# A graph-attention kernel on one core: two groups of nodes share one row of chunks

## The chip, the core and the metric

The kernel runs on one core of a Trainium2 chip. The core has five engines, each with its own queue of instructions that it works through in order: PE (matrix products; the profile lists its weight loads apart, as PEld), DVE (vector work), ACT (activation functions and copies), POOL (general work, and here the issue of gathers), and SP, which issues most plain transfers. They wait for one another by semaphores. Transfers run on 16 DMA engines. PE, DVE and ACT can read and write PSUM, the memory in which matrix products accumulate; all engines work on SBUF. Times are device microseconds of one execution. The time before is 2453.34 us, the median of three runs (2437.25 to 2455.11).

## The reference, cut to what matters

4096 nodes with 512 features pass through three attention layers over one sparse graph. An entry of the adjacency matrix is 1 with a probability that falls with both indices, so low nodes have many neighbours and high ones few. Each layer replaces a node's row by the softmax-weighted mean of its neighbours' projected rows:

```python
x = _layernorm(x + _L0_gnn_ref(x, adj, L0_gnn_W, L0_gnn_a), axis=-1)
x = _layernorm(x + _L1_gnn_ref(x, adj, L1_gnn_W1, L1_gnn_a1, L1_gnn_Wo, L1_gnn_ao, L1_gnn_lin1_w, L1_gnn_lin1_b, L1_gnn_lin2_w, L1_gnn_lin2_b), axis=-1)
...
def _gat_heads(x, adj_mask, W, a):
    Wh = jnp.einsum('nf,hfo->hno', x, W)
    src = jnp.einsum('hno,ho->hn', Wh, a[:, :O])
    dst = jnp.einsum('hno,ho->hn', Wh, a[:, O:])
    e = jax.nn.leaky_relu(src[:, :, None] + dst[:, None, :], ALPHA)
    e = jnp.where(adj_mask[None, :, :], e, NEG)
    attn = jax.nn.softmax(e, axis=-1)
    return jnp.einsum('hnm,hmo->hno', attn, Wh)
...
h = jax.nn.elu(_gat_heads(x, mask, W1, a1))
x1 = jnp.transpose(h, (1, 0, 2)).reshape(x.shape[0], -1)
h2 = _gat_heads(x1, mask, Wo[None], ao[None])[0]
out = jax.nn.elu(h2)
out = jax.nn.relu(out @ lin1_w + lin1_b)
return out @ lin2_w + lin2_b
```

`_L0_gnn_ref` is such a layer with 8 heads of 64, `_L1_gnn_ref` has one with 8 heads of 64 and one with a single head of 512, then two dense products (512 to 1024 to 512). A node without neighbours gets the mean of all rows.

## The kernel before

`sparse_path` works on lists of edges. (`dense_path`, the same computation without lists, runs only if a flag says that some list did not fit.)

**Tiles, groups and chunks.** The 4096 nodes are 32 tiles of 128. A tile has two groups of 64 nodes (`HN`). The edges of a group are laid one after the other into chunks of 128 places. The sizes are set when the program is built: `Part` (line 71) takes the expected number of edges of a group plus 4.2 standard deviations and rounds up to whole chunks, `chunks[h]`; `pairs` is the larger of the two. Tile 0 is cut into four parts by columns, all other tiles are one part, which makes 35 parts. Places that hold no edge are holes. Over all parts the chunks of both groups are 339, the pairs 181. Tile 1 has 12 and 10 chunks, tile 11 5 and 5, tile 31 3 and 3; each part of tile 0 has 9 and 4 or 9 and 5.

**Finding edges** (`find_edges`, line 796). For each part the adjacency rows are turned into signs (ACT), PE makes keys of them (L820, L821), and DVE takes the eight largest over and over (L827, L842), which gives a list of up to `k` neighbours per node. `k` runs from 104 or 112 for tile 0 down to 24. POOL and ACT make degrees (L854), the place at which each node's edges begin (`prs`, a matmul with the triangle `before`, L873) and `s1` (L884): for each chunk a matrix of 128 nodes by 128 places that says which node a place belongs to. Three matmuls per pair of chunks (L902 to L904) then fill `pl`, a PSUM tile with a single buffer, with each place's list, its position in it and its node; L904 adds the constant `own_b`. From `pl` come `nl` (the node of a place), `hole`, and on DVE `sel` and `src`, by which `idx`, the row to be gathered, is made. With `k` under 100 three DVE operations do this for a group of chunks (L912 to L919); in tile 0 there is one operation for each chunk (L925), in 20 groups for its four parts. At the end `limits` (L940, L942) hold the room of each part for the flag. Beside this, `beside(t)` projects tile t for the first layer. The weights of that projection are prepared early by products on POOL (`sprod`, L639) and reductions on DVE (L644). The order of instructions in this stage is set by the build's own scheduler.

**The two head layers** (`heads_layer`, line 1190) run one after the other with the same code, and the order of their instructions is written out by hand. Tiles go from 31 down to 0. The chunks of a tile are cut into units of at most 6 (`GC`): first the pairs that both groups have, then what only one group has. This makes 74 units. For each unit

- `gather` (line 992) has POOL issue one indirect DMA per chunk (L997): 128 rows of the projected table, chosen by `idx`. Rows past the table are left out, so holes move no bytes. There are seven buffers (`GB`), and the gathers of unit i+7 stand behind the work of unit i.
- `weights` (line 1054) makes the attention logits on DVE (`z`, L1065 to L1067: add, leaky maximum, subtract) and their exponents on ACT.
- `add` (line 1082) makes `sm` on DVE (L1093), 128 places by 64 nodes per chunk, multiplies the gathered rows by their weights (`g`, L1124), and sums them on PE into `acc` (L1115), each chunk into the 64 rows of its group.

Once per tile, `spread` (line 1006), two tiles ahead, makes the source nodes' scores of all places on PE and reduces them on DVE (L1035, `ls` L1048). It works in cuts of eight pairs; all cuts but the last are reduced on the spot, the last one later. A finished tile is divided by its sums, gets its layernorm (first layer) or elu (second), and is projected into the table of the next layer (L669). The next layer's gathers begin when the last row of that table is written.

**The third layer** gathers in the same way with four buffers (`GT`), makes `sm` with the weight in it, one DVE operation per chunk (L1102), and works off the two dense products (L1395, L1407) in pieces between the units: `due` grows with the chunks done, at most to 2.5, and each whole number lets a piece go. `fold` finishes a tile when the next tile's first unit is through, `turn` transposes it at the unit after that.

## Time and profile before

The profiled execution took 2276.34 us, with a span of 2274.6 us from its first to its last instruction. All rows below are of this execution.

| stage | us from the span's start | busy PE | DVE | POOL | mean granted clock of PE |
|---|---|---|---|---|---|
| finding edges | 0 to 531 | 367.64 | 379.91 | 220.96 | 0.83 |
| first head layer | 531 to 1016 | 353.61 | 389.48 | 343.62 | 0.90 |
| second head layer | 1016 to 1502 | 362.99 | 331.62 | 354.67 | 0.87 |
| third layer, gathers | 1502 to 2158 | 576.92 | 239.07 | 342.45 | 0.94 |
| third layer, end | 2158 to 2275 | 97.86 | 31.79 | 0.18 | 0.94 |

Over the whole span PE is busy for 1759.0 us, DVE for 1371.9, ACT for 669.2 and POOL for 1261.9. In the profile's lines "out<-in" names what an instruction writes and reads, L997 is a line of the kernel, and "<-" before an engine names what ended a wait. An engine's busy share is an average; whether it sets the pace of a stage is seen from whether it waits there.

### The profile page before, as it was taken

What the parts mean: (1) busy time and instruction counts of PE and PEld (TensorE: products, weight loads), DVE (VectorE), ACT (ScalarE), POOL (GpSimd) and SP (SyncE); (2) the same over time, 40 slices, a digit from 0 to 9 for tenths busy, and PEclk for the clock granted to TensorE, in tenths of its full rate; (3) what the DMA queues carried; (4) which work ended last, traced back from release to release, by engine and by line L of the source; (5) the groups of instructions that cost most, each with busy time, mean ns of one, the idle gap of its engine ahead of it and who ended that gap; (6) DMA issues with size and microseconds to landing.
All of it is one profiled execution on the core that took longest, in us unless ns stands there. A gap on an engine that the chain in (4) does not pass through costs nothing.

```text
span 2274.6 us, 29820 instructions
## 1 busy us (share of the span) xinstructions
PE 1759.0 (77%) x9024; PEld 1033.3 (45%) x9049; DVE 1371.9 (60%) x3750; ACT 669.2 (29%) x2361; POOL 1261.9 (55%) x1816
## 2 busy tenths in 40 slices
PE   3887866673887876756888777638989989898997
PEld 2665532221555554424665444325454544444444
DVE  5887777674999986746787767524242424433423
ACT  3345766664232221102443222012111111111111
POOL 5514443446777777737777777655546544444400
PEclk9898987775999997887999888869989999999999
DMA  6434555543777776625666666455345534434301
GB/s 213 126 113 144 217 201 195 212 148 106 226 229 230 230 221 196 170 78 157 174 174 176 180 186 180 118 167 148 90 139 135 167 103 119 126 99 132 101 19 43
DMA packets 139791, 352.02 MB, mean 155 GB/s; under 512 B 49122, under 2 KB 50154, under 8 KB 135654
## 3 DMA queue, kind: packets, MB, share of 16 engines
q0 software_dynamic: 81360, 206.30, 33.7%
q1 hardware_dynamic: 58262, 143.72, 18.1%
q8 instruction: 75, 1.23, 0.2%
q14 instruction: 94, 0.77, 0.1%
HBM read 371.18 MB, written 42.24 MB: 182 GB/s over the span
## 4 chain that ended last, share of the span: by engine, by line
PE 25%; issue 13%; DVE 13%; DMA 10%; POOL 10%; ACT 1%; POOLq 0%; DVEq 0%; SPq 0%; ACTq 0%
POOL g L997 9%; PE p L1395 9%; DMA g<-table_t,idx 9%; PE acc L1115 9%; DVE g L1124 4%; PE p L1407 3%; PE ph L669 3%; DVE bs L1173 1%; DVE sm L1093 1%; DMA xr<-sx_d 1%; DVE o L1152 1%; DVE z L1065 1%; DVE z L1066 1%; PE pt L655 1%; DVE z L1067 1%
## 5 line engine op out<-in xcount | busy, mean ns | idle before, releaser
L997 POOL DMA_INDIRECT g<-table_t,idx x1017 | 1029.9, 1013 | 558.1 <-issue 253.5
L1115 PE MATMUL acc<-g,sm 128*64 128x260 f32 (+2 forms) x4068 | 608.2, 435 | 252.4 <-DVE g L1124 202.3
L1115 PEld LDWEIGHTS acc<-g,sm 128*64 128x64 f32 x4068 | 351.8, 154 | 482.2 <-DVE g L1124 236.4
L669 PE MATMUL ph<-sw_t,xt 128*128 128x264 f32 (+1 forms) x1536 | 396.1, 407 | 48.0 <-ACT xt L658 36.8
L1124 DVE TENSOR_TENSOR g<-g,wp 128x2048 f32<-128x2048 f32 (+4 forms) x148 | 383.3, 2590 | 12.3 <-ACT wp L1072 12.3
L669 PEld LDWEIGHTS ph<-sw_t,xt 128*128 128x128 f32 x1536 | 295.0, 199 | 113.9 <-ACT xt L658 53.1
L827 DVE MAX8 cand<-key 128x8 f32<-128x24 f32 (+54 forms) x467 | 197.3, 446 | 88.7 <-PE key L821 86.3
L1395 PE MATMUL p<-sht,sl1w 128*128 128x512 f32 (+1 forms) x576 | 229.1, 553 | 0.0
L1407 PE MATMUL p<-sl2w,shid 128*128 128x512 f32 x512 | 228.2, 600 | 0.0
L658 ACT ACTIVATE xt<-pt 128x128 f32<-128x128 f32 x384 | 101.0, 278 | 218.8 <-PE pt L655 218.3
L1065 DVE TENSOR_TENSOR z<-s,g 128x48 f32<-128x48 f32 (+6 forms) x222 | 41.3, 186 | 202.1 <-DMA g<-table_t,idx 199.5
L1395 PEld LDWEIGHTS p<-sht,sl1w 128*128 128x128 f32 x576 | 108.1, 191 | 110.9 <-issue 105.9
L1407 PEld LDWEIGHTS p<-sl2w,shid 128*128 128x128 f32 x512 | 95.6, 191 | 120.1 <-issue 119.3
L820 PE MATMUL key<-sg,s_identb 128*128 128x512 bf16 (+1 forms) x255 | 120.6, 474 | 30.1 <-DVE cand L827 23.2
L682 ACT COPY hrow<-ph 128x260 f32<-128x260 f32 (+2 forms) x194 | 71.0, 373 | 183.0 <-PE ph L669 181.3
L1398 ACT ACTIVATE shid<-p,sl1b 128x512 f32<-128x512 f32 (+1 forms) x72 | 46.0, 639 | 250.7 <-PE p L1395 250.7
L793 ACT ACTIVATE sg<-raw 128x4096 bf16<-128x4096 int32 (+1 forms) x39 | 116.9, 2998 | 9.6 <-PE key L820 5.0
L1102 DVE TENSOR_SCALAR sm<-iota_n,nl,w 128x64 f32<-128x64 f32 x339 | 83.9, 325 | 50.7 <-ACT w L1075 50.7
L821 PE MATMUL key<-frac,places 128*128 128x512 bf16 (+1 forms) x236 | 111.4, 473 | 2.1 <-POOL places L756 2.0
L1169 DVE SCALAR_TENSOR_TENSOR o<-ex,o 128x512 f32<-128x512 f32 x64 | 44.2, 690 | 100.9 <-ACT ex L1168 100.7
L1072 ACT ACTIVATE wp<-z 128x32 f32<-128x32 f32 (+4 forms) x148 | 30.5, 206 | 231.3 <-DVE g L1124 231.1
L658 ACT ACTIVATION_READ_ACCUMULATOR xt<-pt 128x1 f32 x384 | 80.0, 208 | 0.0
(168 smaller groups left out, 1862.9 us busy)
## 6 DMA issues: line engine op xcount, KB each, us to landing
raw<-in_adj_dram SPq DMA_DIRECT2D x31, 2048.0 KB, 7.6
table_t<-hrow SPq DMA_DIRECT2D x64, 260.0 KB, 3.4
xr<-in_x_dram SPq DMA_DIRECT2D x64, 256.0 KB, 4.1
g<-table_t,idx POOLq DMA_INDIRECT x1017
table_t<-hrow SPq DMA_DIRECT2D x32, 257.0 KB, 3.8
sx_d<-o SPq DMA_DIRECT2D x32, 256.0 KB, 3.6
xr<-sx_d SPq DMA_DIRECT2D x32, 256.0 KB, 4.1
out_dram<-xr SPq DMA_DIRECT2D x32, 256.0 KB, 2.8
```

Of the source, the lines that this page charges most:

```text
L658: nc.scalar.activation(xt[:, c, :], pt[:, c, :], AF.Copy, accum_out=st.xparts[:, c, t : t + 1])
L669: nc.tensor.matmul(ph[:n], columns(c), st.w[:, c, j], start=(c == 0), stop=(c == FC - 1))
L793: nc.scalar.activation(sg[:, ts(i, w)], raw[:, ts(i, w)], AF.Sign)
L820: nc.tensor.matmul(out_, ident_b, sg[:, j:e], start=True, stop=False)
L821: nc.tensor.matmul(out_, places[:, w], frac[:, j - w * KW : e - w * KW], start=False, stop=True)
L827: nc.vector.max(out=cand[:, at : at + 8], in_=part)
L997: nc.gpsimd.indirect_dma_start(out=u.g[:, k, : self.st.row], out_offset=None, in_=self.st.table[:, :], in_offset=bass.IndirectOffsetOnAxis ...
L1102: nc.vector.tensor_scalar(sm[:, k], iota_n, node[:, i, h : h + 1], u.w[:, k], op0=OP.is_equal, op1=OP.mult)
L1115: nc.tensor.matmul(out_[h * HN : (h + 1) * HN], sm[:, k], rows(k), start=flags[k][0], stop=flags[k][1])
L1124: nc.vector.tensor_mul(body, body, wp[:, :, :, None].to_broadcast(body.shape))
L1395: nc.tensor.matmul(p1, l1w[:, c, ts(k, P)], hts[b][:, c, :n], start=(c == 0), stop=(c == FC - 1))
L1407: nc.tensor.matmul(p2, hids[b][:, k, ts(j, P)], l2w[:, k, :], start=(k == 0), stop=(k == HC - 1))
```

## The change

The two groups of a part now lie in one row of `n` chunks. Group 0 is laid from the front, group 1 so that it ends at the row's end, beginning in chunk `off`. The chunks in the middle hold edges of both. `n` comes from the edges of both groups together:

```diff
+        room = lambda lam: math.ceil((lam + 4.2 * math.sqrt(lam)) / P)
+        self.n = room(sum(lams))
+        self.chunks = [min(room(lam), self.n) for lam in lams]
+        self.blocks = max(self.chunks)
+        self.off = self.n - self.chunks[1]
```

Over all parts that is 309 chunks, and so 309 gathers per layer, for 339. The parts of tile 0 go from 13 and three times 14 to 12 and three times 13; tile 1 from 22 to 21, tiles 2 to 10 by one each, tile 11 from 10 to 8, tiles 12 and 13 stay at 8, tiles 14 to 19 go from 8 to 7, tiles 20 and 21 from 8 to 6, tile 22 from 7 to 6, tiles 23 to 28 stay at 6, tiles 29 to 31 go from 6 to 5. A chunk in the middle is gathered once and summed twice, so the sums over `sm` and `acc` stay at 339 slots per layer.

A unit takes chunks from the front and from the end; only the last of a part is one run:

```diff
+    def units(self):
...
+        a, b, out = 0, self.n, []
+        steps = math.ceil(self.n / GC)
+        size = min(max(1, round(self.n / steps / 2)), GC // 2)
+        for _ in range(steps - 1):
...
+            out.append(([(a, size), (b - size, size)], list(range(size)), list(range(size, 2 * size))))
+            a, b = a + size, b - size
...
+        out.append((
+            [(a, b - a)],
+            list(range(min(self.chunks[0], b) - a)),
+            list(range(max(self.off, a) - a, b - a)),
+        ))
```

This makes 66 units for 74. Tiles 20, 21 and 22 become one unit of 6 each; tiles 14 to 19 are units of 4 and 3.

In finding edges, `s1` keeps 181 blocks; block i serves chunk i for group 0 and chunk `off` + i for group 1. Group 1's places are counted back from the end (`mids`, `ends_at`). The constant now opens a group of chunks, and the blocks are added to it:

```diff
-                for c in range(m):
-                    chunk = s1[:, (c0 + lo + c) * P : (c0 + lo + c + 1) * P]
-                    nc.tensor.matmul(pl[:, c], chunk, rhs, start=True, stop=False)
-                    nc.tensor.matmul(pl[:, c, :, : k + 1], chunk, rest, start=False, stop=False)
-                    nc.tensor.matmul(pl[:, c, :, k:], ident_b, own_b, start=False, stop=True)
+                nc.tensor.matmul(
+                    pl, ident_b, own_b[:, None, kmax - k :].to_broadcast([P, m, k + 2]), start=True, stop=False
+                )
+                last = None
+                for block, groups, chunks in blocks_in(p, lo, m):
+                    for of, w in ((rhs, k + 2), (rest, k + 1)):
+                        if last:
+                            nc.tensor.matmul(*last, start=False, stop=False)
+                        last = pl[:, chunks, :w], s1[:, ts(p.at + block, P)], of[:, groups, :w]
+                nc.tensor.matmul(*last, start=False, stop=True)
...
-                        for h in range(2):
-                            nc.vector.scalar_tensor_tensor(
-                                sel[:, c, h], iota_k[:, lo + c, :k], kk[:, c, h : h + 1], pl[:, c, h, :k],
+                        nc.vector.scalar_tensor_tensor(
+                            sel[:, c], iota_k[:, lo + c, :k], kk[:, c : c + 1], pl[:, c, :k],
...
+    def blocks_in(p, lo, m):
...
+        for i in range(p.blocks):
+            mine = [(g, c - lo) for g, c in enumerate((i, p.off + i)) if i < p.chunks[g] and lo <= c < lo + m]
+            if len(mine) == 2:
+                out.append((i, slice(0, 2), slice(mine[0][1], mine[1][1] + 1, p.off)))
+            elif mine:
+                g, c = mine[0]
+                out.append((i, slice(g, g + 1), slice(c, c + 1)))
```

The constants by part are filled with one memset for each run of equal values, in place of one or two for each part. A check is added that both groups together fit:

```diff
+        def by_parts(name, of, rows=slice(0, P), rest=None):
...
+            while v < len(pts):
+                e = v
+                while e < len(pts) and of(pts[e]) == of(pts[v]):
+                    e += 1
+                nc.gpsimd.memset(out_[rows, v:e], float(of(pts[v])))
+                v = e
...
-        for v, p in enumerate(pts):
-            nc.gpsimd.memset(limits[0][:, v : v + 1], p.k - 0.5)
-            for h in range(2):
-                nc.gpsimd.memset(limits[1][h * HN : (h + 1) * HN, v : v + 1], float(p.chunks[h] * P))
```

`spread` makes its scores per part in cuts of 20 chunks, three values per head and place in place of four; the holes open the sum and the blocks are added:

```diff
-                pss = self.ps.tile([P, 8, 2, 4, hs], F32, name="pss")
+                pss = self.ps.tile([P, 20, 3, hs], F32, name="pss")
...
+                todo = blocks_in(p, lo, m)
+                for block, groups, chunks in todo:
                     nc.tensor.matmul(
...
-            for lo in cuts[:-1]:
-                collect(lo, scores(lo))
-            last = scores(cuts[-1])
+            cuts = [(p, lo) for p in parts_of(t) for lo in range(0, p.n, 20)]
+            for cut in cuts[:-1]:
+                collect(*scores(*cut))
+            last = scores(*cuts[-1])
```

`weights` adds and subtracts once for each run of a unit, and `add` makes `sm` in two operations, one for each group:

```diff
-            nc.vector.tensor_add(zd, s, d)
+            for at, s in u.pick(self.s[u.t], base):
+                nc.vector.tensor_add(zd[:, at], by(s), d[:, at])
             nc.vector.scalar_tensor_tensor(z, z, ALPHA, z, op0=OP.mult, op1=OP.max)
-            nc.vector.tensor_sub(zd, zd, ls)
+            for at, ls in u.pick(self.ls[u.t], base):
+                nc.vector.tensor_sub(z[:, at], z[:, at], ls)
...
+            for g, slots in enumerate(u.slots):
+                of_g = iota_n[:, g * HN : (g + 1) * HN]
+                if hs > 1:
...
+                    nc.vector.tensor_tensor(
+                        sm[:, at : at + n_],
+                        of_g[:, None, :].to_broadcast(shape),
+                        nl[:, c : c + n_, None].to_broadcast(shape),
+                        op=OP.is_equal,
                     )
```

In the third layer a tile of one unit can now be the last of the order, so what `fold` left is turned after the loop:

```diff
+        if folded:
+            turn(*folded)
         at.inverse(sb, order[-1])
```

## The prediction

> **What bounds the kernel now.** I read the page's groups first, to see what the removed instruction costs, then the busy time by stage, the waits inside each stage, and the order of time on single engines. By their first and last gathers the stages lie at 0 to 531 us (finding edges), 531 to 1016 (first head layer), 1016 to 1502 (second) and 1502 to 2275 (third layer with the dense blocks).
>
> The page's costliest group (busy us, mean ns | idle before, its cause):
>
> ```profile
> L997 POOL DMA_INDIRECT g<-table_t,idx x1017 | 1029.9, 1013 | 558.1 <-issue 253.5
> ```
>
> The answer for its source line (minimum, median and maximum ns of one):
>
> ```profile
> L997 POOL DMA_INDIRECT g<-table_t,idx x1017: 992/998/1527, 533.0 to 2157.2; - x170
> ```
>
> 1017 gathers are 339 per layer. Busy times between the first and last gather of each layer (PE, PEld, DVE, ACT, POOL, granted clock, DMA share, GB/s):
>
> ```profile
> 531.00:983.00 452.00, 332.89 (x2135) 218.72 (x2136) 376.13 (x725) 117.72 (x587) 343.61 (x341) 0.90 0.71 208
> 1016.00:1466.00 450.00, 341.86 (x2143) 222.88 (x2143) 320.06 (x542) 122.88 (x581) 346.75 (x340) 0.88 0.65 172
> 1502.00:2158.00 656.00, 576.92 (x2479) 308.09 (x2480) 239.07 (x891) 110.80 (x264) 342.45 (x340) 0.94 0.44 125
> ```
>
> POOL looks only 76% busy in the first two, but in order of time its gathers stand 0.30 us apart with nothing waited for:
>
> ```profile
> 668.37 0.99 POOL L997 DMA_INDIRECT g<-table_t,idx  x1 [0.30 <-issue]
> 669.67 1.00 POOL L997 DMA_INDIRECT g<-table_t,idx  x1 [0.30 <-issue]
> ```
>
> The pitch is 1.302 us. 339 x 1.302 = 441 us, and gathers ran from 533.0 to 983.0, 450 us: POOL is 98% of that stretch. In the second layer 441 of 447. The waits inside the three stretches confirm it:
>
> ```profile
> POOL g L997 <- PE acc L1115: 7.0, 11, 3.9
> ...
> DVE z L1065 <- DMA g<-table_t,idx: 96.4, 41, 11.2
> ...
> POOL g L997 <- PE acc L1115: 212.0, 47, 11.9
> ```
>
> First layer: POOL waited 7.0 us for buffers. Second: DVE waited 96.4 us for gathers. Third: the reverse, POOL waits 212 us for PE, which is busy 577 of 656 us. So a removed gather is worth up to 1.302 us in two layers and little in the third, as long as DVE, 83% busy in the first layer, keeps up. There it does so only just. For tiles 19 to 14 both take the same time: eight gathers are 10.42 us, and DVE's first weighting (z) of successive tiles starts at 655.0, 665.4 and 675.8, without idle time.
>
> **The change, part by part.**
>
> *Gathers.* 30 fewer per layer: 4 in tile 0, 2 in tiles 11, 20 and 21, 1 in most others, none in 12, 13 and 23 to 28. On POOL 30 x 1.302 = 39.1 us per layer. The bytes do not fall: the gather skips holes. The page's 206.30 MB are 76% of 1017 x 128 rows of 2080, 2080 and 2056 bytes. The same rows come in fewer instructions. I count the full pitch, since 992 to 998 ns hold over half of all gathers, whatever their fill.
>
> The Trainium skill (DMA: Bandwidth & Descriptors, Anatomy of one DMA, SWDGE path) calls descriptor generation small and puts a DMA's fixed time, about 2.0 us, mostly in completion. By it the sum for two layers would be near 0 instead of 78. The rows disagree: POOL is held 1.0 us per gather while earlier ones are still landing.
>
> *DVE in the first layer.* Multiplications by the weights (L1124) take 2.28 us for 4 chunks and 3.35 for 6, 0.535 per chunk: 30 fewer save 16. Units go from 74 to 66; each had three z operations in 0.57 us, a fixed 0.07 in sm and 0.06 in the product: 5.6 saved. 31 units have two runs, so one more add and one more subtract; 128x16 took 0.170, 128x8 0.158, about 0.08 of it under its neighbour: 0.2 per unit, 6.2 added. sm becomes two operations (128x128: 0.285 each, for one 128x256 of 0.418): 0.07 per unit, 4.4 added. The score reductions read 309 x 24 elements, not 362 x 32, at 1.1 ns: 4.6 saved. Fewer inline reductions for tiles 2 and 0 shorten the 17.0 us that DVE waited for PE there, estimated 8. Net -16 - 5.6 + 6.2 + 4.4 - 4.6 - 8 = -24. The product now waits for the same ACT exponents as before, and matmuls on PE keep their number (339 slots), so PE, 333 of 452 us, neither gains nor loses.
>
> The first product chain ended at 991.8. POOL alone would end at 991.8 - 39 = 953. DVE ran from 542.6 to 991.8 with 22 us of waiting for gathers after the first; less 24, and 1.3 earlier by a shorter first unit, it would end near 944. POOL stays last, but the surplus sits early: tiles 14 to 19 need 7 x 1.302 = 9.1 us of POOL and still 10.4 - 0.3 = 10.1 of DVE. POOL runs ahead until its seven buffers stop it. Before tile 11 it has 127 gathers behind it, 533 + 165 = 698 us. By the same prices DVE saves some 9.6 in tiles 31 to 12 (3.5 in the first three, 4.8 in 22 to 20, 1.8 in 19 to 14, less 0.5 in 13 and 12) and gets to tile 11 at 730, not 739.8. After the unit's four gathers (5.2 us) that is a lag of 27 from the end of a gather to its use; the largest in the trace is 20.5. I take off 6 to 8: **-31** for this layer, bounds -39 and -15 (reductions and stalls saving nothing).
>
> *Second layer.* No layernorm, so DVE has 320 of 450 us; its 96.4 us of waiting absorb the gain. PE takes 50.58 us for six tiles of 62.4 us (8.4 each) in the first layer's stretch at clock 1.00, under 9.1. I take **-34**: -39 less 3 for places where DVE or PE is behind, less 2 for a longer last unit (5 chunks, not 4: one more product of 0.5 and eight more matmuls). Bounds -40 and -22: at a lower clock PE would pace tiles 12 to 22, and only 16 gathers, 21 us, would count.
>
> *Edge finding.* Two things sit on DVE, 73% busy up to 200 us. POOL's 105 small memsets (L940 and L942, 11.4 to 22.9 us) stand ahead of the product that DVE waits for:
>
> ```profile
> 12.45 0.20 DVE L827 MAX8 cand<-left 128x8 f32<-128x43 f32 x1
> 24.93 0.69 DVE L644 TENSOR_REDUCE sw_t<-sprod 128x8 f32<-128x512 f32 x1 [12.28 <-POOL sprod L639]
> ```
>
> Now about 55 memsets by runs of equal values, partly between the eight products; a longer iota (2352 elements for 1344, +1.0) and a fill of hole (+0.5) come ahead. The last product should come 2.5 us earlier (0 to 6). The 72 selections of tile 0 (L925, 0.25 us each with its read) become 51, -5.3, and 20 groups become 15. For the other tiles one chunk less of 24 elements is under 0.1 us. Against that, matmuls are put differently into PE's queue (third rival). **-8**, bounds -18 and +8.
>
> *Third layer.* The first three units are one gather shorter, while PE idles 22.2, 3.0 and 2.4 us for them: -3. One inline reduction fewer for tile 0: -1. Tiles 20 to 22 become one unit each; the pacing of dense pieces caps at 2.5, so some move behind the loop, with the same PE time. **-4**, bounds -12 and +6.
>
> Sum: -31 - 34 - 8 - 4 = -77. The profiled execution took 2276.34 us (span 2274.6), giving 2199. The median of the runs shown is 2453.34, 177 us longer; the trace cannot tell where. I carry the difference over unscaled: 2453 - 77 = **2376**.
>
> **The rivals.**
>
> *1. Landing, not issue, sets the gather's price.* Bytes stay, DMA shares of 0.71 and 0.65 rise as the time falls, and a landed row still takes its time. Against it: z starts 1.2 to 1.8 us after the last gather wherever DVE waits. Both head layers would gain nothing: 2453 - 12 = 2441. The skill's sentence above is this rule. Chance 0.09.
>
> *2. DVE and PE take over.* The early lag eats more than 8 us, and the longer timed runs have a lower PE clock. For it: DVE is 96% busy at 626 to 780 us. Against it: z waits of 96.4 us in the second layer. -15 - 22 - 4 - 4 = -45: 2408. Chance 0.16.
>
> The Trainium skill (SBUF: State Buffer, Who interferes with whom) says that DVE instructions with two SBUF inputs block GpSimd instructions that read SBUF; with more z pieces gathers would stretch. The trace shows no such stretch: at 655 to 717 us, with DVE 96% busy, the pitch is 1.302, as at 1016 to 1041 with DVE at 22%.
>
> *3. Slower: PE's queue in edge finding.* The matmul that opens pl (own_b) was the last of each chunk's three; now it opens the group, so it must wait until DVE has read the tile before (one buffer). Behind it queue the next key matmuls, for which DVE waits already (86.3 us). The longest wait now at this place is 4.5 us (PE's loads for pl on POOL s). If each of 31 tiles paid that, +140: 2453 + 140 - 77 = 2516. It decides from 2.5 us per tile (77/31). Against it: the pl of the last tile but one was read by 521.96 us, the next began at 528.49, a slack of 6.5. Chance 0.05.
>
> **How the numbers follow.** The forecast has 0.70. Its bounds are -109 (all best) and -23; scaled by the median the best end is 2336. With rival 2 and 9 us for the runs' own spread (2437 to 2455) the range is **2330 to 2430**, leaving out rivals 1 and 3 and the tails. Faster by over 1% (under 2429; about what a measurement of this kernel tells from no change): 0.70 + 0.16 less 0.01 = 0.85. Within 1%: 0.10. Slower: 0.05.
>
> **What would show it.** Gathers: 927, pitch still 1.30; the first layer's gathers over 405 to 425 us and the second's over 405 to 415, not 450 and 447. DVE's wait for gathers in the second layer falls from 96 to some 55 to 70, POOL's wait for buffers in the first rises from 7 to 10 to 20. The third layer's first gather to the end stays near 770. DVE's 12.28 us stall shrinks. I am wrong if the pitch grows, if tiles 12 to 31 of the first layer are no faster and the later ones do not make it up, or if edge finding passes 540 us.

## The result, and the profile after

The changed kernel took 2323.66 us (median of four runs, 2318.67 to 2328.89) beside 2445.3 us for the kernel before: a ratio of 0.9504, 95% interval 0.9448 to 0.956, or 121.6 us less. The forecast was 77 less. Runs come in sets, each on one chip, and in some sets every kernel is some 7% longer, the one before too (2437 to 2445 us; 2270 to 2273 in the others), so kernels are compared within a set. In two further sets the ratio was 0.9425 (0.9404 to 0.9446; 2141.59 beside 2272.51) and 0.9429 (0.9413 to 0.9445).

The profile of the kernel before that the prediction read (2276 us) belongs to a set of the shorter kind, the first profile of the changed kernel (2329 us) to one of the longer. Stages are therefore compared between two profiles that were taken in one set: the kernel before again (span 2271.6) and the changed kernel again (span 2139.0). Stages run from first gather to first gather, as the traces have them. A third set gave one more profile of each kernel (2267.6 and 2143.6); its differences show how far one pair can be trusted:

| stage, us | before | after | difference | in the third set | forecast |
|---|---|---|---|---|---|
| finding edges | 525.2 | 500.0 | -25.2 | -27.2 | -8 |
| first head layer | 488.2 | 447.4 | -40.8 | -35.5 | -31 |
| second head layer | 483.4 | 442.0 | -41.4 | -41.0 | -34 |
| third layer and dense end | 774.8 | 749.5 | -25.3 | -20.2 | -4 |
| span | 2271.6 | 2139.0 | -132.7 | -124.0 | -77 |

All rows of "after" below are of this profile of 2139.0 us. Its group of gathers on the page (busy us, mean ns, idle before), and the answer for their line (minimum, median, maximum ns):

```profile
L1076 POOL DMA_INDIRECT g<-table_t,idx x927 | 938.5, 1012 | 537.0 <-issue 229.2
```

```profile
L1076 POOL DMA_INDIRECT g<-table_t,idx x927: 992/998/1637, 500.0 to 2008.5; - x186
```

927 gathers, each as long as before. In order of time on POOL they stand 1.30 us apart, as before:

```profile
561.98 0.99 POOL L1076 DMA_INDIRECT g<-table_t,idx  x1 [0.30 <-issue]
563.28 1.00 POOL L1076 DMA_INDIRECT g<-table_t,idx  x1 [0.30 <-issue]
```

Busy times from the first to the last gather of each layer (PE, PEld, DVE, ACT, POOL, granted clock, DMA share, GB/s):

```profile
500.00:914.00 414.00, 324.19 (x2102) 215.91 (x2102) 354.77 (x799) 112.14 (x567) 312.93 (x309) 0.91 0.77 226
947.00:1353.00 406.00, 317.22 (x2115) 213.97 (x2116) 301.05 (x621) 119.13 (x564) 311.63 (x309) 0.92 0.72 191
1389.00:2009.00 620.00, 558.91 (x2415) 286.56 (x2416) 230.21 (x906) 106.75 (x250) 313.75 (x310) 0.95 0.46 129
```

309 gathers at 1.303 us are 403 us, and the first two layers gather for 413.8 and 405.5. The DMA share and the rate rise: the same rows come in less time. The waits in these layers (us in total, times, longest), the first line of the first layer, the second of the second:

```profile
POOL g L1076 <- PE acc L1212: 8.9, 7, 2.5
...
DVE z L1147 <- DMA g<-table_t,idx: 77.5, 36, 10.9
```

The waits of before stand at the same places. The stall of DVE in edge finding has shrunk from 12.3 us to 3.9:

```profile
17.41 0.69 DVE L672 TENSOR_REDUCE sw_t<-sprod 128x8 f32<-128x512 f32 x1 [3.89 <-POOL sprod L667]
```

### The profile page after: what moved, and what is told of

It is laid out like the page before. It is cut to its first block, busy times and chain, and to the rows that moved or that the text cites. A ratio compares the mean times of both kernels' runs of the same rounds, so it can differ in the third digit from the quotient of the medians.

```text
span 2326.7 us, 29282 instructions
## 1 busy us (share of the span) xinstructions
PE 1776.6 (76%) x8987; PEld 1038.4 (45%) x8987; DVE 1328.1 (57%) x3920; ACT 658.9 (28%) x2311; POOL 1161.8 (50%) x1662
## 3 DMA queue, kind: packets, MB, share of 16 engines
q0 software_dynamic: 74160, 206.25, 33.1%
HBM read 347.31 MB, written 42.24 MB: 167 GB/s over the span
## 4 chain that ended last, share of the span: by engine, by line
PE 36%; DVE 12%; issue 9%; another core or an unknown queue 6%; DMA 3%; POOL 3%; ACT 2%; SPq 0%; DVEq 0%; POOLq 0%; ACTq 0%
PE acc L1212 13%; PE p L1475 9%; PE ph L697 6%; PE p L1487 5%; DVE g L1200 4%; POOL g L1076 3%; DMA g<-table_t,idx 2%; DMA xr<-sx_d 1%; PE pt L683 1%; DVE bs L1253 1%; DVE sm L1179 1%; DVE sm L1187 1%; DVE xr L1492 1%; DVE z L1147 1%
## 5 line engine op out<-in xcount | busy, mean ns | idle before, releaser
L1076 POOL DMA_INDIRECT g<-table_t,idx x927 | 937.4, 1011 | 720.1 <-PE acc L1212 352.9
L1212 PE MATMUL acc<-g,sm 128*64 128x260 f32 (+2 forms) x4068 | 619.9, 424 | 219.9 <-DVE g L1200 100.7
L697 PE MATMUL ph<-sw_t,xt 128*128 128x264 f32 (+1 forms) x1536 | 408.4, 415 | 82.1 <-ACT xt L686 46.3
L697 PEld LDWEIGHTS ph<-sw_t,xt 128*128 128x128 f32 x1536 | 303.4, 204 | 154.2 <-ACT xt L686 63.0
L1200 DVE TENSOR_TENSOR g<-g,wp 128x2048 f32<-128x2048 f32 (+3 forms) x132 | 349.1, 2645 | 22.8 <-ACT wp L1155 20.2
L884 DVE MAX8 cand<-key 128x8 f32<-128x353 f32 (+55 forms) x467 | 197.3, 449 | 77.7 <-PE key L878 77.1
L1487 PE MATMUL p<-sl2w,shid 128*128 128x512 f32 x512 | 227.0, 598 | 0.0
L1487 PEld LDWEIGHTS p<-sl2w,shid 128*128 128x128 f32 x512 | 95.4, 190 | 120.1 <-issue 119.3
L877 PE MATMUL key<-sg,s_identb 128*128 128x512 bf16 (+1 forms) x258 | 111.6, 434 | 15.4 <-DVE cand L884 10.1
L1147 DVE TENSOR_TENSOR z<-s,g 128x16 f32<-128x16 f32 (+9 forms) x291 | 43.6, 174 | 92.0 <-DMA g<-table_t,idx 83.7
L1117 DVE TENSOR_REDUCE s<-pss 128x48 f32<-128x144 f32 (+21 forms) x108 | 32.1, 298 | 102.3 <-remote 55.1
```

The lines of the kernel that those rows point to most:

```text
L697: nc.tensor.matmul(ph[:n], columns(c), st.w[:, c, j], start=(c == 0), stop=(c == FC - 1))
L877: nc.tensor.matmul(out_, ident_b, sg[:, j:e], start=True, stop=False)
L884: nc.vector.max(out=cand[:, at : at + 8], in_=part)
L1076: nc.gpsimd.indirect_dma_start(out=u.g[:, k, : self.st.row], out_offset=None, in_=self.st.table[:, :], in_offset=bass.IndirectOffsetOnAxis ...
L1200: nc.vector.tensor_mul(body, body, wp[:, :, :, None].to_broadcast(body.shape))
L1212: nc.tensor.matmul(out_[g * HN : (g + 1) * HN], sm[:, slot], rows(k), start=start, stop=stop)
```

## The experiments

Each kernel is the changed kernel with one edit, unless said otherwise. Times are medians, ratios are to the kernel before of the same set. "Alone" costs are taken against 2141.6 us.

**The two kernels again.** The two first profiles put the kernels the wrong way round (2276 before, 2329 after), against their timed runs.

> The kernel before, unchanged, profiled again. Question: why its first profiled execution (2276) is 170 us under its timed runs (2434 to 2455), while that of the changed kernel (2329) equals them. Theory A (there are stretches in which PE works slowly, as the changed kernel's profile shows at 528 to 562 us and 1063 to 1107 us, and the first profile of the kernel before happened to have none): a profile near 2440 shows such stretches, 100 to 180 us in sum. Theory B (the profile of before is simply shorter than a timed run, and the stretches belong to the changed kernel): again near 2276 without them.

> The changed kernel, unchanged, profiled and timed again beside the kernel before. Theory A: 0.945 to 0.956 of the kernel before; in its profile slow stretches of PE stand at other places or have other lengths than in the first one, and without them the two head layers take 410 to 430 us from first to last gather each. Theory B: the stretches stand at the same places (528, 1063, 1380 us) with the same lengths.

The kernel before took 2273.39 us and its timed runs beside it 2270 to 2275, so its profile is as long as a timed run, and there are no slow stretches in it. Nor are there any in the changed kernel's, which took 2141.59. So B fell: the stretches don't belong to the change. A's guesses at the profile's length and at the ratio (0.945 to 0.956, measured 0.9425) missed, since this set was a short one. Later, on one chip again:

> The kernel before once more, profiled beside the next three. Two sets of runs gave it 2437 to 2445, three gave 2271 to 2273. Theory A (where it takes 2440, its time over 2272 is in stretches in which PE's matmuls follow each other by 1.4 to 2.8 us, in the head layers above all, as in the profile of the version with five steps undone): if this set is a long one, some 70 us more in each head layer, under 25 in the third and none in edge finding; if a short one, stages of 525, 488, 483 and 775 again.

> The changed kernel once more. Theory A: 0.940 to 0.945 of the kernel before in a short set (2142), 0.945 to 0.956 in a long one (2324). Rival (the ratio is set by the chip and not by the change): outside both.

2269.34 and 2141.66, ratio 0.9429 (0.9413 to 0.9445), with stages of 528.4, 482.9, 483.4 and 772.8 before and 501.2, 447.4, 442.4 and 752.6 after. Again a short set: no profile of the kernel before in a long set was had.

**What a gather costs.** In the head layers one more gather behind the last unit of a part, 30 per layer:

```diff
+            if self.dump is not None and len(u.runs) == 1:
+                for _ in range({11: 2, 20: 2, 21: 2, 12: 0, 13: 0}.get(u.t, 0 if 22 < u.t < 29 else 1)):
+                    nc.gpsimd.indirect_dma_start(
+                        out=self.dump.tile([P, F + HS], F32, name="more")[:, : self.st.row],
...
+                        in_offset=bass.IndirectOffsetOnAxis(ap=void, axis=0),
```

> The changed kernel with the 30 gathers put back on POOL in each head layer, but with row numbers beyond the table, so that they move no bytes and nothing waits for them. Theory A (the issue sets the price): each head layer 30 to 39 us longer, the whole 60 to 78 longer. Rival (landing or another engine sets the pace): under 25 us in all.

2214.83 us, ratio 0.9747 (0.9731 to 0.9763): 73 more. The first head layer grew by 27.7 us to 475.1, the second by 37.9 to 479.9. Windows from first to last gather of both layers, in the kernel with the empty gathers:

```profile
500.00:944.00 444.00, 333.28 (x2117) 219.25 (x2118) 359.47 (x807) 113.49 (x570) 341.25 (x338) 0.89 0.73 211
975.00:1420.00 445.00, 332.64 (x2121) 221.31 (x2122) 301.52 (x621) 119.67 (x564) 341.98 (x338) 0.88 0.66 174
```

POOL is busy for 341 us again as in the kernel before, and both layers gather for 444 to 445 us, though DVE has hardly more work than in the changed kernel (359 us for 355). In the second layer 37.9 us for 30 gathers are 1.26 each, nearly the whole pitch of 1.303. In the first they are 0.92 each: some of them fill time in which POOL stood waiting for buffers (8.9 us in the changed kernel, 1.5 here). With real rows:

```diff
-                        in_offset=bass.IndirectOffsetOnAxis(ap=void, axis=0),
+                        in_offset=bass.IndirectOffsetOnAxis(ap=idx[:, u.chunks[-1] : u.chunks[-1] + 1], axis=0),
```

> As the run with 30 empty gathers per head layer, but each of the added gathers fetches its 128 rows of the unit's last chunk once more, into a buffer that nobody reads. The empty ones made the changed kernel 73 us longer (2141.6 to 2214.8). Theory A (the issue on POOL is the whole price): again 2210 to 2220, though 60 x 128 rows of 2 KB, some 15 MB, come on top. Rival (landing adds to the price): 2225 or more, and DVE waits longer for gathers.

2215.63 us, 0.9753 (0.9723 to 0.9782). The page counts 219.10 MB for the gathers' queue, 206.28 with the empty ones, and DVE waits for gathers in all layers for 231.4 and 227.3 us. 12.8 MB more cost 0.8 us, which is no difference that these runs can tell. So the price lies in the issue and not in the landing of the rows.

**DVE in the head layers.** The 30 products that the shared chunks save, put back on a spare tile:

```diff
+                if len(u.runs) == 1:
+                    for _ in range({11: 2, 20: 2, 21: 2, 12: 0, 13: 0}.get(u.t, 0 if 22 < u.t < 29 else 1)):
+                        nc.vector.tensor_mul(
+                            self.spare, self.spare, u.wp[:, 0, :, None].to_broadcast(self.spare.shape)
+                        )
                 nc.vector.tensor_mul(body, body, wp[:, :, :, None].to_broadcast(body.shape))
```

> The changed kernel with the 30 products of one chunk (128x512 by its weights) put back on DVE in each head layer, on a spare tile that nobody reads, ahead of the unit's own product: some 0.6 us each, 18 per layer. Theory A (POOL's issue is the only pace in the head layers, DVE has room): each head layer within 4 us of the changed kernel (447 and 442). Rival (DVE is as near to the limit in the first layer as POOL, so that both had to fall together): the first layer 8 to 18 us longer, the second within 4.

2157.9 us, 0.949 (0.9468 to 0.9512). The rival was right: the first layer took 464.1 us, 16.7 more, the second 442.8, 0.8 more. Its windows up to the last gather of each layer:

```profile
500.00:931.00 431.00, 325.68 (x2106) 221.25 (x2105) 372.13 (x831) 114.82 (x568) 313.40 (x311) 0.90 0.75 219
967.00:1374.00 407.00, 326.22 (x2120) 222.27 (x2121) 317.84 (x650) 118.88 (x564) 312.80 (x309) 0.90 0.72 191
```

DVE's 17.4 us (372.1 for 354.8) lengthen the first stretch of gathers by 13.9 us (427.7 for 413.8) and the stage by 16.7, although DVE is busy for only 86% of it. In the second, with DVE at 74% and then 78%, as much work more costs nothing. So the first layer has two paces at once. 30 gathers put back cost 27.7, DVE's products 16.7, and its full gain could only be had because both fell.

**Edge finding.** First the number of small memsets, 105 for the constants of room, one per part:

```diff
-            while e < len(pts) and of(pts[e]) == of(pts[v]):
+            while e < len(pts) and not (each and e > v) and of(pts[e]) == of(pts[v]):
```

> The changed kernel with the three constants of room (room_k, room_n, room) filled by one memset per part, 105 in place of about a third of that. Theory A (the memsets ahead of the products on POOL delay edge finding, since DVE waits for the products): the first gather comes 10 to 25 us later than in the changed kernel unchanged, and the time rises by as much. Rival (edge finding is shorter by its 21 fewer selections and its differently ordered matmuls, not by the memsets): within 4 us.

2142.07 us, first gather at 500.8: no cost, and so not the price of 105 memsets. Then the same number in the order that the kernel before had:

```diff
+        limits = [big.tile([P, nv], F32, name=f"limits{i}") for i in range(2)]
+        for v, p in enumerate(pts):
+            nc.gpsimd.memset(limits[0][:, v : v + 1], p.k - 0.5)
+            for h in range(2):
+                nc.gpsimd.memset(limits[1][h * HN : (h + 1) * HN, v : v + 1], (p.chunks[0] * P, 2.0 * N * longest)[h])
```

> The changed kernel with the constants of room filled as before: 105 memsets, of which two of three stand on the same tile in turn. The run with 105 memsets one after the other for three tiles cost nothing (0.03 us each there; 0.11 us each in the kernel before, where they waited for one another). Theory A: DVE's longest wait for the product of weights is again some 8 us longer (12 for 4) and edge finding ends 4 to 6 us later, as DVE's time in this stage adds up. Rival (what DVE loses early it makes up later): under 2 us.

2155.99 us, 0.9485 (0.9464 to 0.9507): 14.4 more, and the first gather comes at 511.5, 11.5 later. POOL in order of time, first in the kernel with 105 memsets one after the other, then in this one:

```profile
19.27 0.86 POOL L831 MEMSET room_k<- 128x1 f32 x23
```

```profile
19.46 0.10 POOL L1001 MEMSET limits<- 128x1 f32 x1
19.50 0.24 POOL L1003 MEMSET limits<- 64x1 f32 x2
19.79 0.10 POOL L1001 MEMSET limits<- 128x1 f32 x1
```

23 memsets in 0.86 us there; three in 0.33 us here, where two of every three start only when the one before has ended. And DVE's wait for the products here (us, times, longest):

```profile
DVE sw_t L672 <- POOL sprod L667: 21.2, 15, 12.6
```

The long wait is back at 12.6 us, and 10.1 us more of waiting for the products (21.2 for 11.1) end the stage 11.5 us later, about twice the 4 to 6 expected. Nothing is made up. The edit overdoes it, though: in the kernel before these waits were 16.5 us, since all products came behind the memsets there and two come ahead of them here. What the change itself saved at this place is 5.4 us of waiting (7.0 in the third set), not 10.1.

The selections of tile 0, 72 for 51:

```diff
-                    for c in range(m):
+                    twice = (5 if p.first else 6) if lo == 0 else 0
+                    for c in list(range(m)) + [0] * twice:
```

> The changed kernel with 72 selections in tile 0 for 51 (21 done twice, same operands, same result). A selection with its read takes 0.33 + 0.08 us in the profile by its duration, but the next starts 0.35 us after it. Theory A (DVE paces tile 0's four parts): the first gather comes 5 to 9 us later. Rival (those parts are paced by PE or POOL, and DVE has room): under 2 us.

2154.13 us, 0.9483 (0.9463 to 0.9503), first gather at 511.5: 11.5 us later, where 5 to 9 were expected. DVE's own work is 4.9 us of that (busy for 376.2 us in this stage, not 371.3), 0.23 for each of the 21. A selection's rows last 0.32 and 0.08 us, but they overlap, and the next selection starts 0.24 us after it (the 0.35 of the expectation is a misreading):

```profile
50.71 0.32 DVE L986 SCALAR_TENSOR_TENSOR sel<-iota_k,kk,pl 128x104 f32<-128x104 f32 x1
50.96 0.08 DVE L986 DVE_READ_ACCUMULATOR sel<-iota_k,kk,pl 128x1 f32 x1
50.96 0.32 DVE L986 SCALAR_TENSOR_TENSOR sel<-iota_k,kk,pl 128x104 f32<-128x104 f32 x1
```

The other 6.6 us are waiting, nearly all of it for keys (83.3 us for 76.9). How the one leads to the other was not looked into, and in eleven profiles of kernels that leave edge finding alone the first gather comes between 499.4 and 505.6, so that single microseconds can't be told here.

The constant that opens pl, in pieces of two chunks:

```diff
-                nc.tensor.matmul(
-                    pl, ident_b, own_b[:, None, kmax - k :].to_broadcast([P, m, k + 2]), start=True, stop=False
-                )
+                for c in range(0, m, 2):
+                    e = min(c + 2, m)
+                    nc.tensor.matmul(
+                        pl[:, c:e], ident_b, own_b[:, None, kmax - k :].to_broadcast([P, e - c, k + 2]),
+                        start=c == 0, stop=False,
+                    )
```

> The changed kernel with the constant own_b laid into pl two chunks at a time, as the kernel before did for each pair, in place of once per group: about 165 matmuls for 50, some 14 us more on PE in edge finding. Theory A (the stage's chain goes through DVE's waits for pl and for the keys behind it on PE's queue): the first gather 3 to 10 us later. Rival (PE's share of the work is covered): under 2 us.

2139.07 us, first gather at 501.3: nothing. PE's time for pl is covered in this stage, DVE's isn't.

**The third layer.** Shorter units:

```diff
+        if short and self.n == 7:
+            size = 3
...
+            if short and t in (20, 21, 22):
...
+                    Unit(t, [(at, 4)], [[k for k in s if k < 4] for s in u.slots]),
+                    Unit(t, [(at + 4, 2)], [[k - 4 for k in s if k >= 4] for s in u.slots]),
```

> The changed kernel with short second units in the third layer alone, as the kernel before had them: tiles 20 to 22 cut into 4 and 2 chunks, tiles 14 to 19 into 6 and 1. Theory A (PE waits for the weights of a short unit that comes right behind a long one, and this is where the third layer's 25 us came from, 749 for 775): the third layer takes 8 to 15 us more. Rival (the layer gains by fewer gathers or by the pacing of the dense pieces, not by the units): within 3 us.

2158.17 us, the layer 15.9 longer (765.4). But the expectation has two faults. The kernel before had units of 4 and 4 in tiles 12 to 21, and last units of one chunk only in tiles 22, 7, 3 and 2, so this isn't the old cut but another one. And in tiles 20 to 22 it parts sums of the two groups that otherwise start together on PE: the same 1356 matmuls of the sums take 210.4 us of PE's time, not 199.4 (6.6 of the 11 more in these three tiles), and PE is busy for 681.9 us, 10 more. Some 6 us are left for waits. The other way, with three buffers of 8 in place of four of 6 and 50 units for 66:

```diff
-GT = 4
+GT = 3
+GCT = 8
...
-        units = units_of(order)
-        at = Attention(st2, gp, wk, pacc, ps)
+        units = units_of(order, GCT)
+        at = Attention(st2, gp, wk, pacc, ps, GCT)
```

> The changed kernel with units of up to 8 chunks in the third layer and three gather buffers of 8 in place of four of 6 (the same memory): tiles 12 to 19 become one unit each. Theory A (each second, short unit costs PE 1.5 to 2 us, as nine more of them cost 16): the third layer 8 to 16 us shorter than 749. Rival (fewer buffers make PE wait for gathers, or the pacing of dense pieces sets it): 0 or longer.

2109.46 us, 0.928 (0.9256 to 0.9303): 32 less, and the third layer 721.8 for 749.5, 27.7 less where 8 to 16 were expected. PE's busy time and waits from the third layer's first gather to the end: before, after, and with units of 8 (three kernels, windows first, then the waits of the latter two):

```profile
1497.00:2272.00 775.00, 676.34 (x2779) 359.14 (x2779) 271.08 (x980) 129.19 (x306) 341.35 (x339) 0.94 0.39 110
```

```profile
1389.00:2139.00 750.00, 671.91 (x2778) 343.84 (x2778) 270.37 (x1016) 127.89 (x298) 314.27 (x310) 0.95 0.40 114
```

```profile
1389.00:2109.90 720.90, 659.91 (x2778) 337.53 (x2778) 260.95 (x936) 125.37 (x282) 311.55 (x309) 0.96 0.43 118
```

```profile
PE pt L1452 <- DVE o L1249: 28.9, 8, 4.3
PE acc L1212 <- DMA g<-table_t,idx: 21.1, 2, 20.8
PE acc L1212 <- DVE sm L1187: 17.8, 18, 4.5
```

```profile
PE acc L1214 <- DVE sm L1189: 38.6, 22, 18.9
PE pt L1454 <- DVE o L1251: 8.5, 3, 3.0
```

The same 2778 matmuls (one more in the count before). PE stands idle for 98.7 us with 74 units, 78.1 with 66 and 61.0 with 50, and its own busy time falls by 4.4 (by 0.3 in the third set) and 12.0. Of the 12.0 the sums make 9.1 (199.4 to 190.3). With 50 units PE waits far less for the previous tile's o at a transpose (8.5 us for 28.9). The expectation's first rival, that three buffers would make it wait for gathers, is out. Its second, the pacing of the dense pieces, is not. PE at tile 11 before, and after (where the line L1487 is a dense piece):

```profile
1639.30 1.96 PE L1115 MATMUL acc<-g,sm 128*64 128x257 f32 x16
1645.52 1.11 PE L1372 MATMUL pt<-s_ident,o 128*128 128x128 f32 x4 [4.26 <-DVE o L1169]
```

```profile
1532.66 7.13 PE L1487 MATMUL p<-sl2w,shid 128*128 128x512 f32 x16
1539.63 0.60 PE L1452 MATMUL pt<-s_ident,o 128*128 128x128 f32 x4
```

Behind the first unit of a tile PE turns the previous tile's o, which DVE has yet to finish. Where a dense piece comes in between, PE works on that for 7 us; where none does, it stands. The wait at the transpose in the first unit's wake, in us, at seven tiles, in the order in which they are worked (22 and 21, which end the order, are left out):

| tile | 74 units | 66 units | 50 units |
|---|---|---|---|
| 1 | 3.7 | 3.7 | 3.0 |
| 11 | 4.3 | 0, a piece | 0, a piece |
| 2 | 3.7 | 3.5 | 0, a piece |
| 12 | 4.4 | 4.3 | 0, a piece |
| 3 | 4.3 | 4.3 | 0, a piece |
| 4 | 4.5 | 4.3 | 0, a piece |
| 5 | 4.3 | 3.7 | 0, a piece |

Larger units let `due` grow more at once, so that a piece falls due right behind the first of them. From 66 to 50 units nearly 21 us go here (23.8 to 3.0), more than the 17.1 that PE's idle time falls by in all: elsewhere some came back. That units and pieces could be told apart by a run that moves the pieces alone was not tried.

**Together.** Four steps undone at once: the empty gathers, the chained memsets, the selections and the short units of the runs above.

> The changed kernel with four steps undone at once: the 30 empty gathers per head layer, the room constants by 105 chained memsets, the 21 selections and the short units of the third layer. Alone they cost 73, 14, 12.5 and 16.5 us, 116 in sum. Theory A (the four are independent and make up nearly the whole difference of 131): 2250 to 2262, edge finding 520 to 525. Rival (two of them cover one another): 2240 or less.

2251.88 us, 0.9913 (0.9891 to 0.9934), first gather at 524.1: the four nearly add up (110 of 116). And the products of the head layers on top, in five steps:

> The four steps undone at once and the 30 products on DVE per head layer on top, that is nearly all that the change takes away (not: the additional pieces of z and sm, the order of own_b). With four undone it took 2251.9, 19.7 us under the kernel before, 9 of it in the first head layer, 6 in the second, 8 in the third, 1 in edge finding. Theory A (what is missing in the first head layer is DVE's time, as the products alone cost 16.7 us there with fewer gathers): the first head layer 485 to 492 for 479, the whole 2258 to 2268. Rival (with the gathers back POOL is the only pace again, and DVE's products are covered): 2250 to 2256.

This run fell into a long set: 2439.59 us beside 2436.96, ratio 1.0001 (0.9976 to 1.0025). The gain is gone. Beside the 2271.6 us of the set before, A's 2258 to 2268 are 0.994 to 0.998 and just touch this interval, the rival's 2250 to 2256 (0.990 to 0.993) do not; but in a long set neither the times in us nor the stages can be held against the forecast, and so DVE's share in the first layer is not shown by this run. Its empty gathers also differ a little: one each at tiles 11 to 13, 20, 21 and 23 in place of two at 11, 20 and 21, into one buffer in place of two. The equality is a little flattering: two of the five weigh more than what they undo (some 5 us in the memsets, 10 in the unpaired sums), and stand for smaller terms that were left in.

**Units of 8 everywhere.** The last edit with the head layers' seven buffers of 6 turned into five of 8:

```diff
-GC = 6
-GB = 7
+GC = 8
+GB = 5
```

> The version with units of up to 8 chunks in all three layers: in the head layers five gather buffers of 8 in place of seven of 6 (40 chunks for 42). The run with 8 in the third layer alone took 2109.5. Theory A (DVE stands at its limit in the first head layer, and each unit less saves it some 0.7 us of fixed cost): the first head layer 4 to 10 us shorter than 447, the second within 4 of 439 to 442, the whole 2100 to 2106. Rival (fewer buffers: POOL waits for them, a unit's product comes later): 2112 or more.

In that same long set: 2270.43, ratio 0.9329 (0.9296 to 0.9362). So that it could be judged, both versions side by side:

> Units of up to 8 chunks in the third layer once more, beside those with 8 in all layers: 0.928 of the kernel before in a short set, 0.93 to 0.945 in a long one.

> Units of up to 8 in all three layers once more, to compare with 8 in the third layer alone on the same chip. Theory A (DVE stands at its limit in the first head layer): 4 to 10 us less than those. Rival (fewer buffers cost as much): the same or more.

2112.48 (0.9303, 0.9288 to 0.9319) and 2130.49 (0.9386, 0.9367 to 0.9406). The rival was right: with five larger buffers the head layers take 453.4 and 454.6 us, not 447.4 and 441.5. The best version is the changed kernel with units of 8 in the third layer alone, 29 to 32 us under it.

## Why the prediction came out 45 us short

The direction and the reason held, each of the four terms was too small, and the result lies 6 us below the range. Of what the prediction named to watch, the 927 gathers at 1.30 us, the two stretches (413.8 and 405.5) and the smaller stall came as said; DVE's wait in the second layer (77.5, forecast 55 to 70), POOL's wait for buffers (8.9, forecast 10 to 20) and the third layer (749.5, forecast near 770) did not.

*Gathers, -39.1 per layer.* Right. Both stretches shrank by that in the pair of the table (452.9 to 413.8 and 445.6 to 405.5; by 33.7 and 38.0 in the third set), and the runs with empty and with real gathers show that the issue is the price. The Trainium skill (DMA: Bandwidth & Descriptors, Anatomy of one DMA, SWDGE path) calls descriptor generation a small part of a DMA's time; by that sentence the two layers would have gained near nothing. The runs disagree: up to 1.26 us per gather that moves no bytes. With that, the first rival is out.

*First head layer, -31.* The step that failed is "I take off 6 to 8". Its reason is there: DVE came to tile 11 when it was forecast to (197.2 us after the first gather; 730 - 533 is 197), and POOL waited for buffers, so that the lag from a unit's last gather to its z stopped at 19.5 us (15.6 before) and never came to 27. But the kernel before pays for buffers too. Its waits in three profiles, and the changed kernel's 8.9 and 8.0 beside them:

```profile
POOL g L997 <- PE acc L1115: 9.8, 11, 5.4
```

That is the set of the table; 7.0 stood in the profile that I had read out myself, 4.4 in the third set. What stands on both sides isn't taken off the difference. How much was left to take off differs by the pair: nothing in the table's (-39.1 for the gathers, -40.8 with what DVE does behind the last one), some 5 us in the third set (-33.7 and -35.5). The layer after took 447.4 us both times, the layer before 483 to 488. "POOL stays last" was half the truth: the products put back on DVE alone cost 16.7 us. DVE's own saving (-24 forecast, -21 in its busy time) was not a reserve but the second half of what was needed. So the second rival named a real danger, which did not come about, because the change took as much off DVE as off POOL.

*Second head layer, -34.* Measured -41.4 (-41.0 in the third set), beyond its bound of -40. The step that failed is the 3 us for places where an engine is behind and the 2 for a longer last unit: DVE still waits 77.5 us for gathers (94.7 before), so that work was covered and cost nothing, as the products put back there cost nothing (0.8 us).

*Edge finding, -8.* A large miss, -25.2 (-27.2 in the third set), below its bound of -18. DVE is busy 9.4 us less in this stage (380.7 to 371.3). Of that the 21 selections are 5.1, as forecast, and the three operations of the other tiles (L912 to L919) 3.1 (42.1 to 39.0), the 0.1 per tile that was left out as nothing. The rest, nearly 16, is waiting, and there lies the step that failed: apart from the stall for the product, put at 2.5, the prediction took DVE's waits as they stood. DVE waited 5.4 us less for products (16.5 to 11.1), 5.1 less for keys (82.0 to 76.9), 4.4 less for nl in the other tiles (9.6 to 5.2) and 2.8 less at the selections of tile 0 (21.3 to 18.5), while small waits grew by some 2. That waiting here grows with POOL's memsets and with DVE's own work is shown by the two runs above, 11.5 us each. Why the waits for keys and nl fell is not shown.

*Third layer, -4.* The step "tiles 20 to 22 become one unit each ... with the same PE time" counted PE's work and not its idle time. The work did stay (4.4 us less, 0.3 in the third set), but PE's idle time fell by 21 (20 in the third set). Of that the trace shows 5 before tile 27 (3 forecast) and 8 at tiles 11 and 23, where a dense piece now fills a wait of 4.3 us each: "some move behind the loop" priced where the pieces went, not what they cover where they come to lie. The rest is in pieces of under 3. At the tiles that lost a unit themselves (0 to 3, 7 and 20 to 22) idle time fell by 4 in all. So the number of units worked through the places of the pieces, as far as the runs show it, and little by the changes of unit as such.

*The third rival.* PE, which only writes pl, did wait for its readers on DVE (7.9 us, where there had been 1.5), but DVE waited less for keys than before (76.9 for 82.0). It never came near the 2.5 us per tile from which it would decide.

*The 177 us.* I carried the difference over unscaled to a set that was 7% longer. It came to 122 there and 128 to 131 in the short sets, so that this choice was sound, but by luck: nothing in the trace that it rested on told of the two kinds of sets.

## What to carry to other kernels

Before a loss is taken off a gain, look whether the kernel before pays it already: only what changes between the two counts, and one profile of a kernel may not tell how large it is (4.4, 7.0 and 9.8 us here). An engine that is busy for 86% of a stretch can set its pace together with one that is taken up for 97% of it (309 gathers at 1.303 us in 413.8); work put back on each of them alone shows this in two runs. Where an engine works off two kinds of work in a fixed order, look at what lies in each of its waits: a change that moves a piece of one kind into a wait of the other gains the wait, though no work went away.

## What the runs showed of the hardware

**Stretches of slow matmuls.** In the long sets PE has stretches in which matmuls follow each other far too slowly with nothing waited for. PE in order of time in the changed kernel's first profile (span 2326.7), with a window of a longer stretch:

```profile
551.89 0.59 PE L1212 MATMUL acc<-g,sm 128*64 128x260 f32 x1 [1.50 <-issue]
554.68 0.59 PE L1212 MATMUL acc<-g,sm 128*64 128x260 f32 x1 [2.20 <-issue]
557.48 0.59 PE L1212 MATMUL acc<-g,sm 128*64 128x260 f32 x1 [2.21 <-issue]
```

```profile
1063.00:1107.00 44.00, 17.68 (x42) 7.99 (x43) 10.90 (x17) 3.08 (x15) 30.63 (x31) 0.50 0.53 142
```

42 matmuls in 44 us, where the second layer of the short set has 2115 in 406. The granted clock is 0.50 throughout, but half the clock alone explains 0.43 us from one of these matmuls to the next, as the same trace has them elsewhere, not 1.4 to 2.8. The head layers lose most: 532.1 and 524.8 us in this profile for 447.4 and 442.0, the third layer 770.2 for 749.5, edge finding nothing (499.7 for 500.0). The version with five steps undone shows such stretches as well (560.7 and 558.3 us in its head layers). The Trainium skill (TensorE: Matmul & The Clock Gate, Seeing it yourself) tells of a clock stuck at a quarter for over 50 us; the records here say 0.50. The chip numbered 8 on record had a short set and 48 minutes later a long one, so the chip alone does not decide it. What starts these stretches, and why whole sets are free of them, stays open.

**Memsets.** One after the other on POOL they stand under 0.04 us apart (23 in 0.86 us). Where two of every three wait for the end of the one before, three take 0.33 us.

**Empty gathers and the counters.** With 60 empty gathers the gathers' queue moves 0.03 MB more (206.28 for 206.25), though it counts 4800 packets more (78960 for 74160), 80 for each gather, as for the full ones. The page's HBM reads rise by 16.0 MB (363.28 for 347.31), the same as with 60 full ones (363.28), whose queue moves 12.8 MB more. 60 x 128 rows of 2080 bytes are 15.97 MB: this counter goes by the rows that a gather names, moved or not, and the queue's by those that move. It also fell by 23.9 MB from the kernel before (371.18) to the changed one, whose queue moves the same bytes.
